# Softmax maxima turned for two chunks at once, and a second pass two rounds later

## The chip, the cores and the metric

The kernel runs on one core of a Trainium2 chip, in one launch. The time is that of one execution on the device, in microseconds (us). The core's engines work side by side, each through its own queue and in order: TensorE (PE, matrix products, with the loading of weights shown apart as PEld), VectorE (DVE), ScalarE (ACT), GpSimd (POOL) and SyncE (SP, which here only issues transfers). They wait for each other through semaphores.

## The reference

The input x has 16 sequences of 512 tokens with 256 features, in float32. One transformer block is computed, in which attention and the feed-forward part both read the same normalised input:

```python
xn = _layernorm(x, axis=-1)
x = x + _L0_attn_ref(xn, Wq, Wk, Wv, Wo) + _L0_ffn_ref(xn, router_w, router_bias, gate_w, up_w, down_w, sgate_w, sup_w, sdown_w)
```

Attention has 16 heads of 16 features, rotary embedding on q and k, a causal mask and a softmax:

```python
q, k = _rope(q, k)
scores = jnp.einsum('bqhd,bkhd->bhqk', q, k) * scale
scores = jnp.where(causal, -jnp.inf, scores)
attn = jax.nn.softmax(scores, axis=-1)
out = jnp.einsum('bhqk,bkhd->bqhd', attn, v).reshape(B, S, H * Dh)
return out @ Wo.T
```

The feed-forward part routes each of the 8192 tokens to 4 of 32 experts (gate, up and down matrices of 128 hidden features, SiLU), weighs their outputs by the softmax of the router, and adds a shared expert of 512 hidden features that every token passes.

## The kernel before

**Rounds.** The whole kernel is one list of steps that the program writes out by hand, and the engines' queues follow that order. Its beat is the round: 20 rounds a sequence, 10 for each pair p (0 and 1) of head chunks. A chunk c is four heads, laid out in 128 partitions, 32 for each head: 16 features and spare rows (`HP = 32`, `DH = 16`). `qts[b]` and `kts[b]` hold the turned q and k of sequence b with the chunks side by side, so pair p has chunks 2p and 2p+1. Sequence b begins its first pass in round 20b, and there are 320 such rounds.

**Two passes of scores.** In each round `scores(r)` (line 815) gives PE two interleaved sets of small products. The first pass multiplies q by k for two heads of one block arrangement (`BLOCKS_Q`) into the PSUM tile `sq`; DVE then takes the causal maximum of each query row (line 821, output `junk`, with the maximum itself going to `top`). The second pass works `LAG` = 10 rounds behind: k by q, turned the other way, into `sk`, where a 17th row of the operands subtracts the maximum: row `DH` of k holds -1 and row `DH` of q holds the maximum. ACT then takes the exponential (line 829, `pe`) and POOL clears what lies above the diagonal (line 841). The tiles `sq` and `sk` have one buffer each, so the next round's first pass waits until DVE has read `sq`.

**Maxima.** `maxima(b, p, c)` (lines 847 to 852) turns the four tiles `top[c]` on PE (four transposes into `pm`, line 850) and adds the result to chunk 2p+c of q on DVE (line 852, `qt<-qt,pm`). It runs for c = 0 in the pair's 8th round (20b + 10p + 7) and for c = 1 in the second round after the pair's ten (20b + 10p + 11). In the second pass the pair's chunk 0 is first read in round 20b + 10p + 10 and chunk 1 in round 20b + 10p + 14.

**Events.** Everything else of attention stands in a table of events by round: `values` (line 861, `po`, the exponentials by v), `normalized` (877 to 881, `pot`), `turned` (894, `pto`), `finish` (909, `pa`, the output projection), and for the next sequence `fetch` (line 157, the transfer of `axt`), `project` (741, `pqk`, followed on DVE by four operations of the rotary embedding, lines 751 to 761), `turn_heads` (779, `pt`) and `project_v` (769, `pv`). Each event has an estimated PE cost.

**Filling.** The feed-forward part fills the rounds. Until round 130 that is the shared expert (line 227 `psgu`, gate and up; 239 `psd`, down), from round 130 to 301 the routed experts (629 `pxt`, turn the rows; 642 `pg`, gate and up; 666 `py`, down), then the last halves of the shared expert, with the sums of the output (line 720). The routing itself runs in the first 34 rounds. The main loop gives each round as much filling as levels the estimated PE cost between two boundaries, the last of which is `full`; in a round the scores come first, then filling steps and events by turns, and events that are left over last. The gated unit behind `psgu` and `pg` costs ACT a tanh (line 260) and DVE two operations (262, 263); behind `pg` DVE also prepares the weights and numbers of the rows (`four`, `wrow`, `who`, lines 652 to 660).

```python
if r >= LAG:
    bk, sk = divmod(r - LAG, 20)
...
owed = owed + level - busy[r] if r < full else 1e9
```

Of the kernel before, what the change touches and what calls it, by code (L numbers as in the profile page):

```python
# [11 lines left out]
F32 = mybir.dt.float32  # L12
# [10 lines left out]
P = 128  # L23
# [22 lines left out]

LAG = 10
ROUNDS = B * 2 * 10  # L50
BLOCKS_Q = [[(0, 2, 0), (0, 0, 384)], [(0, 1, 0), (1, 1, 256)], [(0, 3, 0)], [(1, 3, 0)], [(1, 2, 0), (1, 0, 384)]]
BLOCKS_K = [[(0, 0, 0)], [(0, 1, 0), (0, 3, 384)], [(0, 2, 0), (1, 2, 256)], [(1, 0, 0)], [(1, 1, 0), (1, 3, 384)]]
# [17 lines left out]
def block_kernel(ctx: ExitStack, tc, x, wqkv, wo, rope, rw, rb, wexp, sg, su, sd, out):  # L70
# [64 lines left out]
    def bank(shape, name):  # L135
# [11 lines left out]
    ]  # L147

    top = [
        [fixed.tile([P, P], F32, tag=f"top{c}{i}", name=f"top{c}{i}") for i in range(NT)]  # L150
        for c in range(2)
    ]
    axts = {}

# [3 lines left out]

    def constant_heads(i):
        nc.vector.memset(qk[i], 0.0)  # L160
        nc.vector.memset(qk[i][:, NH:, DH : DH + 1], -1.0)

    def constant_values(s):
        for i in range(NT):
# [1 line left out]
            nc.gpsimd.memset(va[s][i][:, :, DH : DH + 1], 1.0)  # L166

    def constant_maxima():
        for c in range(2):
            for i in range(NT):  # L170
                nc.gpsimd.memset(top[c][i], 0.0)

    work = ctx.enter_context(tc.tile_pool(name="awork", bufs=2))

# [611 lines left out]
    def scores(r):  # L786

        jobs = []
        if r < ROUNDS:
            b, s = divmod(r, 20)  # L790
            p, s = divmod(s, 10)
            g0 = 0 if s % 2 == 0 else 2
            sq = ps_q.tile([P, 2, S], F32, tag="q", name=f"sq_{r}")
            jobs.append([
                (sq[:, h, col : col + (i + 1) * P],
                 qts[b][(g0 + h) * HP : (g0 + h) * HP + DH, 2 * p + c, i * P : (i + 1) * P],
                 kts[b][(g0 + h) * HP : (g0 + h) * HP + DH, 2 * p + c, : (i + 1) * P])
                for c, i, col in BLOCKS_Q[s // 2] for h in range(2)
            ])
        if r >= LAG:  # L800
            bk, sk = divmod(r - LAG, 20)
            pk, sk = divmod(sk, 10)
            k0 = 2 if sk % 2 == 0 else 0
            st = ps_k.tile([P, 2, S], F32, tag="k", name=f"sk_{r}")
            jobs.append([
                (st[:, h, col : col + S - k * P],
                 kts[bk][(k0 + h) * HP : (k0 + h) * HP + DH + 1, 2 * pk + c, k * P : (k + 1) * P],
                 qts[bk][(k0 + h) * HP : (k0 + h) * HP + DH + 1, 2 * pk + c, k * P :])
                for c, k, col in BLOCKS_K[sk // 2] for h in range(2)
            ])  # L810
        for n in range(max(len(job) for job in jobs)):
            for job in jobs:
                if n < len(job):
                    dst, lhsT, rhs = job[n]
                    nc.tensor.matmul(dst, lhsT=lhsT, rhs=rhs, start=True, stop=True)  # L815
        if r < ROUNDS:
            for c, i, col in BLOCKS_Q[s // 2]:
                n = (i + 1) * P
                for h in range(2):
                    at = (g0 + h) * HP + DH  # L820
                    nc.vector.tensor_tensor_reduce(  # L821
                        out=junk[:, :n], in0=sq[:, h, col : col + n], in1=causal[:, S - n :],
                        scale=1.0, scalar=LOWEST, op0=ALU.add, op1=ALU.max,
                        accum_out=top[c][i][:, at : at + 1],
                    )
        if r >= LAG:
            j = sk // 2
            pe = work.tile([P, 2, S], F32, tag="pe", name=f"pe_{r}", bufs=8)
            nc.scalar.activation(pe, st, AF.Exp, scale=DH ** -0.5)  # L829
            uncut.append((pe, j))  # L830
            pes[bk, pk, j, k0 // 2] = pe
# [12 lines left out]
                )  # L844
        uncut.clear()

    def maxima(b, p, c):
        pt = bank([P, S], f"pm_{b}_{p}_{c}")
        for i in range(NT):
            nc.tensor.transpose(pt[:, i * P : (i + 1) * P], top[c][i], ident)  # L850
        dst = qts[b][:, 2 * p + c, :]
        nc.vector.tensor_tensor(dst, dst, pt, ALU.add)

    pos_o = {}

# [94 lines left out]
    for b in range(B):  # L950
        for p in range(2):
            r = 20 * b + 10 * p
            at(r + 7, 0.45, lambda b=b, p=p: maxima(b, p, 0))
            at(r + 11, 0.45, lambda b=b, p=p: maxima(b, p, 1))
            for c, rv in ((0, r + LAG + 7), (1, r + LAG + 11)):
                at(rv, 2.3, lambda b=b, p=p, c=c: values(b, p, c))
                at(rv + 1, 0.45, lambda b=b, p=p, c=c: normalized(b, p, c))
            at(r + LAG + 13, 0.45, lambda b=b, p=p: turned(b, p))
# [185 lines left out]
```

## Time and profile before

| | us |
|---|---|
| median of 3 runs | 1840.01 |
| their range | 1839.31 to 1848.48 |
| the profiled execution's own time | 1840.64 |
| its span, first to last instruction | 1838.9 |
| PE busy | 1761.6 |
| scores, `sq` and `sk`, each matmul's mean | 0.466 and 0.467 |
| 256 transposes of maxima, busy time | 42.1 |
| 64 additions to q on DVE, busy time | 43.9 |

[...] In the timeline the columns are start, duration, engine, line, operation, output<-inputs, shape and count; a bracket at the end tells how long the engine had been idle before and what ended it. In the list of groups, the busy time and the mean in ns follow the bar, then the idle time before them. The mean granted clock of PE was 0.978.

### The profile page before, as it was taken

The numbers are of one execution on the slowest core, as the hardware profiler recorded it, in microseconds if no ns is written. First come the engines' busy times: TensorE is split into PE (matmuls) and PEld (weight loads), VectorE is DVE, ScalarE is ACT, GpSimd is POOL, SyncE is SP. The second block draws the span as 40 slices with busy tenths as digits, with TensorE's granted clock in tenths as the row PEclk, the third lists the DMA queues.
The fourth block names the chain that finished last, engine by engine and source line by source line (L and its number), as shares of the span: only waits on it lengthen the run. The fifth ranks groups of instructions, "written<-read, shape, count | busy, mean of one in ns | idle before, by whom it ended". The sixth has DMA issues, their size and how long they took to land.

```text
span 1838.9 us, 38201 instructions
## 1 busy us (share of the span) xinstructions
PE 1761.6 (96%) x13489; PEld 1297.5 (71%) x13489; DVE 1227.4 (67%) x4278; ACT 847.2 (46%) x1481; POOL 1015.9 (55%) x1336
## 2 busy tenths in 40 slices
PE   7888889999999999899999999999999999999988
PEld 5655557777776777677777787777777787777654
DVE  6888676766766666465766666666665656666784
ACT  2355433333333333255555555555555555555332
POOL 3334317767767767345666565565655665656311
PEclk9988899999999999899999999999999999999999
DMA  4644335555544433478889898888988888897797
GB/s 154 209 155 160 111 121 172 187 185 174 188 162 143 154 124 121 152 187 230 212 201 229 208 234 206 224 208 209 238 200 230 208 217 223 200 247 159 204 305 235
DMA packets 230832, 353.24 MB, mean 192 GB/s; under 512 B 23408, under 2 KB 166512, under 8 KB 230640
## 3 DMA queue, kind: packets, MB, share of 16 engines
q1 hardware_dynamic: 168176, 262.83, 45.2%
q0 software_dynamic: 55296, 76.86, 21.4%
q10 hardware_dynamic: 7168, 11.09, 1.7%
q8 instruction: 107, 1.75, 0.4%
q14 instruction: 85, 0.70, 0.1%
HBM read 220.74 MB, written 131.01 MB: 191 GB/s over the span
## 4 chain that ended last, share of the span: by engine, by line
PE 85%; DVE 9%; DMA 2%; ACT 2%; issue 1%; SPq 1%; ACTq 0%; POOL 0%; DVEq 0%
PE pg L642 15%; PE sq L815 13%; PE psgu L227 11%; PE po L861 7%; PE py L666 7%; PE pqk L741 5%; PE psd L239 5%; PE sk L815 4%; PE pxt L629 4%; PE pt L779 3%; PE pa L909 3%; PE pv L769 3%; DVE junk L821 2%; PE pm L850 2%; PE pot L877 1%
## 5 line engine op out<-in xcount | busy, mean ns | idle before, releaser
L680 POOL DMA_INDIRECT moe<-yb,who x288 | 449.9, 1562 | 301.5 <-DMA moe<-yb,who 120.1
L821 DVE CUSTOM_DVE_ANT_0 junk<-sq,causal 128x384 bf16<-128x384 f32 (+3 forms) x1024 | 502.8, 491 | 153.3 <-PE sk L815 117.7
L829 ACT ACTIVATE pe<-sk 128x1024 f32<-128x1024 f32 x320 | 327.8, 1024 | 332.0 <-PE sk L815 264.8
L841 POOL TENSOR_SCALAR_AFFINE_SELECT pe<-pe 128x256 f32<-128x256 f32 x512 | 262.5, 641 | 271.1 <-ACT pe L829 268.3
L815 PE MATMUL sq<-kt,qt 16*128 16x384 f32 (+3 forms) x2048 | 369.8, 466 | 18.6 <-DVE top L821 18.5
L815 PE MATMUL sk<-qt,kt 17*128 17x512 f32 (+3 forms) x2048 | 369.9, 467 | 1.8 <-ACT pe L829 1.8
L535 POOL DMA_INDIRECT xs<-rows,pos x256 | 250.6, 979 | 82.6 <-issue 66.9
L642 PEld LDWEIGHTS pg<-xbt,w 128*128 128x128 f32 x2304 | 275.4, 193 | 26.8 <-ACT yb L674 9.4
L642 PE MATMUL pg<-xbt,w 128*128 128x128 f32 x2304 | 289.8, 279 | 2.5 <-DMA w<-in_wexp 2.5
L815 PEld LDWEIGHTS sq<-kt,qt 16*128 16x128 f32 x2048 | 175.9, 186 | 147.8 <-issue 41.6
L815 PEld LDWEIGHTS sk<-qt,kt 17*128 17x128 f32 x2048 | 176.3, 186 | 10.2 <-ACT pe L829 2.8
L262 DVE SCALAR_TENSOR_TENSOR gs_e<-th_e,pg 128x256 f32<-128x256 f32 x144 | 60.7, 421 | 169.8 <-ACT th_e L260 160.0
L861 PE MATMUL po<-pe,va 128*32 128x512 f32 (+3 forms) x2048 | 157.3, 449 | 0.0
L666 PE MATMUL py<-w,ht 128*128 128x256 f32 x576 | 152.3, 387 | 0.0
L227 PE MATMUL psgu<-sxt,sg_sb 128*128 128x256 f32 x496 | 140.9, 408 | 4.9 <-DMA sxt<-xt_d 3.3
L674 ACT ACTIVATE yb<-py,wrow 128x256 f32<-128x256 f32 x288 | 121.3, 474 | 31.9 <-PE py L666 31.4
L227 PE MATMUL psgu<-sxt,su_sb 128*128 128x256 f32 x496 | 131.5, 389 | 0.0
L861 PEld LDWEIGHTS po<-pe,va 128*32 128x32 f32 x2048 | 61.2, 112 | 99.6 <-issue 78.3
L260 ACT ACTIVATE th_e<-pg 128x256 f32<-128x256 f32 x144 | 55.3, 384 | 160.6 <-PE pg L642 160.6
L239 PE MATMUL psd<-sd_sb,hs 128*128 128x256 f32 x512 | 127.2, 392 | 0.4 <-DVE hs L263 0.4
L260 ACT ACTIVATE th_s<-psgu 128x256 f32<-128x256 f32 x128 | 49.1, 384 | 159.3 <-PE psgu L227 154.6
L227 PEld LDWEIGHTS psgu<-sxt,sg_sb 128*128 128x128 f32 x496 | 89.3, 196 | 38.5 <-issue 15.7
(148 smaller groups left out, 2491.1 us busy)
## 6 DMA issues: line engine op xcount, KB each, us to landing
w<-in_wexp SPq DMA_DIRECT2D x288, 384.5 KB
xb<-xs SPq DMA_DIRECT2D x144, 265.0 KB
sum<-moe SPq DMA_DIRECT2D x48, 256.0 KB
xn_d<-xn SPq DMA_DIRECT2D x16, 530.0 KB
rows<-xn_d SPq DMA_DIRECT2D x16, 530.0 KB
xt_d<-xt ACTq DMA_DIRECT2D x32, 256.0 KB
moe<-none SPq DMA_DIRECT2D x16, 512.0 KB
sxt<-xt_d SPq DMA_DIRECT2D x31, 256.0 KB
```

The costliest lines, as they stand in the source:

```text
L227: nc.tensor.matmul(ps[:, u, :], lhsT=w[:, c, m * P : (m + 1) * P], rhs=hold["xt"][:, c, :], start=(c == 0), stop=(c == 1),)
L239: nc.tensor.matmul(hold["py"][:, il, :], lhsT=hold["h"][:, m, il * P : (il + 1) * P], rhs=sd_sb[:, m, :], start=(m == 0), stop=(m == HS // ...
L535: nc.gpsimd.indirect_dma_start(out=views[n % NVIEWS], out_offset=bass.IndirectOffsetOnAxis(ap=index, axis=0), in_=row, in_offset=None,)
L642: nc.tensor.matmul(pg[:, u, c * HB : (c + 1) * HB], lhsT=w[n][:, c, at : at + H], rhs=rows[:, dc, c * HB : (c + 1) * HB], start=(dc == 0), ...
L666: nc.tensor.matmul(py[:, c, :], lhsT=h[:, c * P : (c + 1) * P], rhs=w[n][:, c, 2 * D : 3 * D], start=True, stop=True,)
L674: nc.scalar.mul(yb[:, c, :], py[:, c, :], weight[:, c : c + 1])
L680: nc.gpsimd.indirect_dma_start(out=moe[c], out_offset=bass.IndirectOffsetOnAxis(ap=at[:, c : c + 1], axis=0), in_=yb[:, c, :], in_offset=N ...
L815: nc.tensor.matmul(dst, lhsT=lhsT, rhs=rhs, start=True, stop=True)
L821: nc.vector.tensor_tensor_reduce(out=junk[:, :n], in0=sq[:, h, col : col + n], in1=causal[:, S - n :], scale=1.0, scalar=LOWEST, op0=ALU.a ...
L829: nc.scalar.activation(pe, st, AF.Exp, scale=DH ** -0.5)
L841: nc.gpsimd.affine_select(out=diag, in_=diag, compare_op=ALU.is_ge, fill=0.0, base=0, pattern=[[0, 2], [1, P]], channel_multiplier=-1,)
L861: nc.tensor.matmul(po[g * HP : (g + 1) * HP, k * P :], lhsT=va[b % 2][k][:, 8 * p + 4 * c + g, :], rhs=pes[b, p, j, g // 2][:, g % 2, col ...
```

## The change

Both chunks of a pair now share one set of tiles. The maxima of chunk c go to column `DH + c` of a head's 32, so four transposes turn both chunks, and one addition adds both rows to both chunks of q. Chunk c of k has its -1 in row `DH + c` and zero in the other, so that each chunk subtracts its own maximum; the second pass reads 18 rows. `top` is now kept by pair instead of by chunk. The single call per pair is in round 20b + 10p + 11, after all ten rounds of its first pass. The second pass runs 12 rounds behind, and `values`, `normalized`, `turned` and `finish`, which are placed by `LAG`, move by two rounds with it. The next sequence's `fetch`, `project`, `turn_heads` and `project_v` get other rounds, and the boundary `full` is written by `LAG` (328; it was 326).

```diff
-LAG = 10
+LAG = 12
...
-        nc.vector.memset(qk[i][:, NH:, DH : DH + 1], -1.0)
+        chunks = qk[i][:, NH:, :].rearrange("p (k h) e -> p k h e", h=4)
+        for c in range(2):
+            nc.vector.memset(chunks[:, c::2, :, DH + c : DH + c + 1], -1.0)
...
-                 kts[bk][(k0 + h) * HP : (k0 + h) * HP + DH + 1, 2 * pk + c, k * P : (k + 1) * P],
-                 qts[bk][(k0 + h) * HP : (k0 + h) * HP + DH + 1, 2 * pk + c, k * P :])
+                 kts[bk][(k0 + h) * HP : (k0 + h) * HP + DH + 2, 2 * pk + c, k * P : (k + 1) * P],
+                 qts[bk][(k0 + h) * HP : (k0 + h) * HP + DH + 2, 2 * pk + c, k * P :])
...
-                    at = (g0 + h) * HP + DH
+                    at = (g0 + h) * HP + DH + c
...
-                        accum_out=top[c][i][:, at : at + 1],
+                        accum_out=top[p][i][:, at : at + 1],
...
-    def maxima(b, p, c):
-        pt = bank([P, S], f"pm_{b}_{p}_{c}")
+    def maxima(b, p):
+        pt = bank([P, S], f"pm_{b}_{p}")
         for i in range(NT):
-            nc.tensor.transpose(pt[:, i * P : (i + 1) * P], top[c][i], ident)
-        dst = qts[b][:, 2 * p + c, :]
-        nc.vector.tensor_tensor(dst, dst, pt, ALU.add)
+            nc.tensor.transpose(pt[:, i * P : (i + 1) * P], top[p][i], ident)
+        dst = qts[b][:, 2 * p : 2 * p + 2, :]
+        nc.vector.tensor_tensor(dst, dst, pt.unsqueeze(1).to_broadcast([P, 2, S]), ALU.add)
...
-            at(r + 7, 0.45, lambda b=b, p=p: maxima(b, p, 0))
-            at(r + 11, 0.45, lambda b=b, p=p: maxima(b, p, 1))
+            at(r + 11, 0.45, lambda b=b, p=p: maxima(b, p))
...
-            at(20 * b + 6, 0.0, lambda b=b: fetch(b + 1))
-            for i, r in enumerate((9, 12, 15, 19)):
+            at(20 * b + 7, 0.0, lambda b=b: fetch(b + 1))
+            for i, (r, rv) in enumerate(((10, 22), (12, 24), (16, 25), (18, 26))):
...
-                at(20 * b + 22 + i, 0.9, lambda b=b, i=i: project_v(b + 1, i))
+                at(20 * b + rv, 0.9, lambda b=b, i=i: project_v(b + 1, i))
...
-    last, full = ROUNDS + LAG + 16, ROUNDS + 6
+    last, full = ROUNDS + LAG + 16, ROUNDS + LAG - 4
```

More of the change, by code (lines that the diff above doesn't have):

```diff
@@ L149, in block_kernel @@
     top = [
-        [fixed.tile([P, P], F32, tag=f"top{c}{i}", name=f"top{c}{i}") for i in range(NT)]
-        for c in range(2)
+        [fixed.tile([P, P], F32, tag=f"top{p}{i}", name=f"top{p}{i}") for i in range(NT)]
+        for p in range(2)
     ]
@@ L168, in constant_maxima @@
     def constant_maxima():
-        for c in range(2):
+        for p in range(2):
             for i in range(NT):
-                nc.gpsimd.memset(top[c][i], 0.0)
+                nc.gpsimd.memset(top[p][i], 0.0)
     work = ctx.enter_context(tc.tile_pool(name="awork", bufs=2))
```

## The prediction

> **What bounds the kernel now.** I read the page's busy times first, then the same by stage, then single rounds in the timeline.
>
> ```profile
> span 1838.9 us, 38201 instructions
> PE 1761.6 (96%) x13489; PEld 1297.5 (71%) x13489; DVE 1227.4 (67%) x4278; ACT 847.2 (46%) x1481; POOL 1015.9 (55%) x1336
> ```
>
> TensorE (PE) works 96% of the span, VectorE (DVE) 67%. The next view splits the span at the stages: before the 34th round, with the shared expert as filling, with the routed experts, rounds 302 to 319. Columns: window, time, then busy us of PE, PEld, DVE, ACT, POOL, granted clock, DMA share, GB/s.
>
> ```profile
> 37.30:261.00 223.70, 189.18 (x1345) 127.80 (x1344) 172.65 (x736) 100.47 (x207) 77.83 (x231) 0.90 0.43 143
> 261.00:770.00 509.00, 498.48 (x3436) 356.05 (x3432) 345.15 (x1046) 180.86 (x277) 343.21 (x441) 0.99 0.48 159
> 770.00:1704.00 934.00, 931.21 (x7776) 718.90 (x7780) 593.46 (x2202) 512.98 (x918) 551.92 (x557) 0.99 0.85 214
> 1704.00:1787.00 83.00, 73.81 (x555) 51.02 (x548) 64.82 (x177) 28.54 (x41) 18.97 (x34) 0.96 0.83 259
> ```
>
> In the two long stages (1443 us) PE is all but never idle (498.48 of 509, 931.21 of 934): a microsecond of PE work removed there is a microsecond won, a microsecond of PE waiting added is one lost. At the two ends DVE is the busier of the two for its stage (77% and 78%) and PE has gaps. The third view is one round of the expert stage, round 167.
>
> ```profile
> 974.20 0.69 PE L815 MATMUL sq<-kt,qt 16*128 16x512 f32 x1
> ...
> 975.27 2.05 PE L642 MATMUL pg<-xbt,w 128*128 128x128 f32 x16
> 975.40 0.69 DVE L821 CUSTOM_DVE_ANT_0 junk<-sq,causal 128x512 bf16<-128x512 f32 x1 [0.49 <-PE sk L815]
> ...
> 976.75 0.08 DVE L821 DVE_READ_ACCUMULATOR2_ANT top<- 128x1 f32 x1
> ...
> 977.26 2.36 PE L861 MATMUL po<-pe,va 128*32 128x512 f32 x32
> ...
> 977.84 0.42 DVE L262 SCALAR_TENSOR_TENSOR gs_e<-th_e,pg 128x256 f32<-128x256 f32 x1 [1.01 <-ACT th_e L260]
> ...
> 979.10 0.17 DVE L660 COPY who<-xb 128x2 int32<-128x2 int32 x1
> ...
> 979.55 0.66 PE L629 MATMUL pxt<-ident,xb 128*128 128x128 f32 x4
> ...
> 980.04 0.60 PE L850 MATMUL pm<-ident,top 128*128 128x128 f32 x4
> ...
> 980.57 0.18 PEld L815 LDWEIGHTS sq<-kt,qt 16*128 16x128 f32 x1 [0.17 <-issue]
> ...
> 980.68 0.69 DVE L852 TENSOR_TENSOR qt<-qt,pm 128x512 f32<-128x512 f32 x1 [1.41 <-PE pm L850]
> ```
>
> It holds PE's prices, from start to next start: the round's scores 1.07 us (974.20 to 975.27), values 2.29, the transposes of maxima 0.53 here (0.44 to 0.45 where a like set of four follows another). Likewise in other rounds: pg 1.78, py 0.87, four pxt 0.44, one psgu 1.73, half a psd 0.91, pqk 1.72; joins between blocks add about 0.2 us a round (166: scores, pg, pxt, py sum to 4.16, the round took 4.35). It also shows DVE's clockwork when pg comes right after the scores: maxima done 2.6 us after the round's start (3.0 with four pieces), then gate work until 979.27, which is 5.07 us after it. And it shows L852, the addition to q, ending at 981.37, 0.8 us after the next round's scores have begun. Today nobody misses it: those rows are read three rounds later.
>
> **The change part by part.** *Maxima once per pair.* 32 of the 64 sets of four transposes go: 32 x 0.45 = 14.4 us of PE (by 0.44 and 0.53: 14.1 to 17.0). One wide addition of 128x1024 stands for two of 128x512. No row has that shape; these bound it:
>
> ```profile
> L850 PE MATMUL pm<-ident,top 128*128 128x128 f32 x256 | 42.1, 287 | 0.0
> L852 DVE TENSOR_TENSOR qt<-qt,pm 128x512 f32<-128x512 f32 x64 | 43.9, 687 | 60.0 <-PE pm L850 59.9
> L881 DVE TENSOR_TENSOR ot<-pot,rs 128x256 f32<-128x256 f32 x64 | 27.2, 424 | 2.2
> ```
>
> Doubling 256 to 512 adds 263 ns, so 1024 takes 687 + 2 x 263 = 1213 ns; below lies 687 (nothing for the second half), above 2 x 687 = 1374. I take 1.21. The 18th row of the second pass is free: 16 and 17 rows cost the same 1.07 us.
>
> *Lag twelve.* Two more rounds hold the first pass alone and two more the second alone. A round with one pass still took 1.06 us in the trace, so 332 instead of 330 blocks cost 2 x 1.06 = 2.1 us. Together PE's work falls by 12.3 us.
>
> *The new wait.* This is the heart. The addition is issued in round 20b+11 (first pair) or 20b+21 (second), and the second pass of that pair begins in the very next round; before there were three rounds between. The second matmul in PE's queue for that round needs the whole addition, PE works in order, and behind it stand the rest of the scores and all that follows. On DVE the addition is queued behind the round's maxima and behind the gate work of any block that PE was given before the transposes. In the first pair's case a projection was also issued one round earlier (pqk is last in round 20b+10). What this costs DVE is seen in round 170, whose scores began at 991.45:
>
> ```profile
> 991.21 0.69 DVE L751 TENSOR_TENSOR tcos<-pqk,rope_sb 128x512 f32<-128x512 f32 x1
> ...
> 992.89 0.62 DVE L761 TENSOR_TENSOR qk<-tcos,tsin 128x256 f32<-128x256 f32 x1
> 993.44 0.55 DVE L821 CUSTOM_DVE_ANT_0 junk<-sq,causal 128x384 bf16<-128x384 f32 x1
> ...
> 995.18 0.08 DVE L821 DVE_READ_ACCUMULATOR2_ANT top<- 128x1 f32 x1
> ```
>
> The maxima end 3.8 us into that round instead of 3.0; with pqk last they end at about 3.95. So I go through the 32 places with the order in which the changed program issues its instructions, compare when DVE ends (plus 0.1 for the signal) with when PE comes to the next scores, and call the difference the stall.
>
> Expert stage, 18 places. Second pair, pg ahead of the transposes: gate work to 5.07, addition to 6.3, scores possible at 6.4; PE (scores, pg, pxt, pm, py, joins) is there at 4.8: 1.6 us each in rounds 141, 261, 281; in 301 py comes twice, 1.2; in 241 another pg covers it. First pair, pg ahead: 3.95 + 1.45 gate work + 1.21 + 0.1 = 6.7 against 4.8: 1.9 each in 211 and 231, 0.1 in 191 under another pg. First pair, no pg ahead: 5.25, and up to 0.75 more where gate work of the round before is queued ahead of the projection, against 4.4 to 5.67: 0.7 (131), 0.75 (151, 291), 1.05 (171), 0.8 (271), none in 251. Second pair, no pg ahead (161, 181, 201, 221): 4.3 against 4.8 or more, none. Sum 14.0 us. If the addition took 0.69 it would be about 8, with 1.37 and the slower rows of the gate work (0.75 for 0.35) about 20.
>
> Shared stage, 9 places, psgu in pg's stead (gate work ends at 4.4): 1.35 (61), 0.55 (81, 121), 0.65 (41), none (101), 0.9 (51, 91), 0.95 (71, 111): 6.8 us, 3 to 10 by the same bounds.
>
> Start, 3 places (11, 21, 31). There the routing's DVE work (some 3 us) stands ahead of the addition too; gross 2.5 to 5 us each, but PE already loses about 45 us in these rounds to such chains, and one delay hides another. I take 4, bounds -4 and 12.
>
> End. In rounds 305 to 319 DVE, with the sums of the output, is the slower engine, so that the same work of PE spread over two more rounds leaves more for after round 320: 6 us more PE work there by the order, 2.5 less before; I take 2 (0 to 6). Rounds 311 and 321 have only psgu and psd around the transposes: 2 us of waiting each, 4 (0 to 7).
>
> *Moved steps.* The load of axt is issued a round later, and so is its first reader, three rounds on as before; it waits for the last project_v, one round earlier in both. On SP it passes a round's stores and loads, none of which waits for it. turn_heads writes the other kt one round after its last reader instead of two, in PE's own order. I cost these at nothing: three rounds are over 14 us; if the load were late, up to 5 us a sequence.
>
> Sum: -14.4 + 2.1 + 14.0 + 6.8 + 4 + 2 + 4 = +18.5 us on the profiled execution's 1840.64 us (span 1838.9 and 1.7 around it), 0.63 above the median shown: 1858.5 for the median; I say 1858.
>
> [...]
>
> **The rivals.** *The saving shows, the wait does not* (20%): the addition runs earlier than I queue it, or PE's joins swallow the lateness. For it: PE has 0.8 us pauses that nobody explains, and DVE is 36% idle there. Against: DVE works in order and the rows above leave it 1 to 2 us late. Price: 1840.0 - 14.4 + 2.1 = 1828. The point that decides is the sum of stalls: under 3.1 us the change is faster by over 0.5%.
> *It cancels* (18%): stalls between 3.1 and 21.5 us, because the start and the end give nothing and the expert stage is at its lower bound, 8 + 3: 1839; with the evener spread of values, projections and finishes some of PE's present gaps before the scores go as well.
> *The ends get worse* (12%, slower too): DVE-bound rounds at both ends pay in full, 12 + 13 us for my 10: 1873.
> *Forecast* (50%): 1846 to 1870.
>
> **The numbers.** 0.5% (9.2 us) is about what a measurement of this kernel can tell from no change. Faster 0.20, within 0.18, slower 0.62. The range goes from the saving's case, 1829, to 1871; the likeliest case has 1846 to 1870.
>
> **What would show it.** In the changed profile: pm x128 and about 14 us less; the addition near 1.21 us; the waits of second-pass scores (sk) on DVE's qt, near nothing now, at some 20 us or more in about 20 places, the rounds after 20b+11 and 20b+21 lengthened where pg stands before pm; PE no longer 100% busy in the expert stage. Were sk to wait for qt under 5 us in all, my prediction is wrong and the time falls to 1828.

## The result and the profile after

The changed kernel took 1897.97 us in the median of four runs (1892.49 to 1902.74) against 1839.66 of the kernel before beside it (1837.45 to 1848.48): 1.0296 times as long, 95% interval 1.0268 to 1.0323. It is slower, as forecast, but by 58 us where 18.5 had been worked out, and lies above the stated range, which ended at 1871 us.

First the busy times of the changed kernel's page, then busy times by stage: before round 34, the shared expert as filling (to round 130), the routed experts (to round 302), rounds 302 to 319, the rest. Columns: window, time, busy us of PE, PEld, DVE, ACT, POOL, granted clock, DMA share, GB/s.

```profile
span 1896.2 us, 37958 instructions
PE 1788.5 (94%) x13361; PEld 1311.4 (69%) x13361; DVE 1220.2 (64%) x4248; ACT 844.0 (45%) x1481; POOL 1013.9 (53%) x1336
```

```profile
37.00:276.00 239.00, 193.77 (x1266) 126.57 (x1268) 169.48 (x722) 94.41 (x199) 74.59 (x225) 0.84 0.39 132
276.00:795.00 519.00, 502.80 (x3428) 361.08 (x3430) 342.08 (x1032) 182.35 (x282) 342.93 (x442) 0.99 0.47 156
795.00:1745.00 950.00, 939.55 (x7737) 723.64 (x7733) 593.30 (x2200) 512.54 (x920) 550.05 (x557) 0.99 0.85 211
1745.00:1834.00 89.00, 76.10 (x524) 50.95 (x526) 64.35 (x175) 28.09 (x41) 21.70 (x35) 0.90 0.79 245
1834.00:1896.20 62.20, 51.46 (x304) 31.54 (x296) 27.94 (x55) 17.32 (x22) 9.98 (x20) 0.88 0.61 200
```

The same cut through the kernel before, first, fourth and fifth stage:

```profile
37.30:249.50 212.20, 180.95 (x1297) 121.43 (x1296) 168.81 (x725) 97.51 (x202) 77.06 (x229) 0.90 0.44 148
...
1706.30:1789.20 82.90, 73.71 (x533) 51.03 (x532) 66.22 (x182) 28.02 (x41) 18.32 (x34) 0.96 0.85 267
1789.20:1838.90 49.70, 41.52 (x257) 24.32 (x256) 26.06 (x49) 14.71 (x19) 8.10 (x16) 0.92 0.75 238
```

PE has 128 matmuls fewer and is busy 27 us longer. In the first stage it ran 31 matmuls fewer and was still busy for 12.8 us more, at a granted clock of 0.84 instead of 0.90; it was idle 45 us and not 31. In the trace the granted clock of PE stands at half in blocks of 3.4 us. Such blocks make up 41 us of the first stage before and 75 after, and 15 and 32 us from round 302 on; in the two long stages they are the same, 24 us together.

Against the prediction by stage, with round starts from both traces and the prediction's PE work split by the order in which the programs issue it:

| stage | before | after | change | predicted |
|---|---|---|---|---|
| to round 34 | 249.5 | 275.8 | +26.3 | +1.8 (work -2.2, waits 4) |
| to round 130 | 515.2 | 518.9 | +3.7 | +1.1 (work -5.7, waits 6.8) |
| to round 302 | 941.5 | 950.2 | +8.7 | +6.4 (work -7.6, waits 14.0) |
| to the end | 132.6 | 151.2 | +18.6 | +9.2 (work 3.2, 2 + 4 for the end) |

The two long stages, where nearly all of the working went, came out 5 us above the forecast. The two short ends hold 45 of the 57 us.

The wait itself is there. This is the group of the new addition in the changed kernel (duration in ns as min/median/max), with what waited for it:

```profile
L855 DVE TENSOR_TENSOR qt<-qt,pm x32: 1208/1216/1222, 116.4 to 1842.0; 128x1024 f32<-128x1024 f32 x32
its engine sat idle before it (us, times) until:
  PE pm L853: 1.0, 2
who waited for it (us, times):
  PE sk L818: 17.4, 11
  PEld sk L818: 9.5, 3
```

The addition took 1.216 us for 1.21 predicted, and second-pass scores on PE waited for it 17.4 us at 11 places (PEld's 9.5 us are mostly two of the same waits, in rounds 12 and 22, seen at the loading of weights). One such place, round 232, in the timeline:

```profile
1353.29 0.49 PE L853 MATMUL pm<-ident,top 128*128 128x128 f32 x3
...
1355.01 0.69 PE L818 MATMUL sq<-kt,qt 16*128 16x256 f32 x2
1355.05 0.42 DVE L266 SCALAR_TENSOR_TENSOR ht<-gs_e,pg 128x256 f32<-128x256 f32 x1
...
1355.39 0.35 DVE L655 SCALAR_TENSOR_TENSOR four<-xb,w 128x4 f32<-128x4 f32 x2
...
1355.92 1.21 DVE L855 TENSOR_TENSOR qt<-qt,pm 128x1024 f32<-128x1024 f32 x1
...
1357.28 0.66 PE L818 MATMUL sk<-qt,kt 18*128 18x512 f32 x1 [1.58 <-DVE qt L855]
```

The transposes ended at 1353.8, but DVE came to the addition only at 1355.92, after the maxima and the gate work of a block (gs_e, ht, four). PE started the round at 1355.01, issued one pair of first-pass matmuls and stood until 1357.28, 0.15 us after the addition's end: scores longer by 2.27 us. That is the mechanism as predicted.

### The profile page after: what moved, and what is told of

The parts are those of the page before. It is cut to its first block, busy times and chain, and to the rows that moved or that the text cites. A ratio compares the mean times of both kernels' runs of the same rounds, so it can differ in the third digit from the quotient of the medians.

```text
span 1896.2 us, 37958 instructions
## 1 busy us (share of the span) xinstructions
PE 1788.5 (94%) x13361; PEld 1311.4 (69%) x13361; DVE 1220.2 (64%) x4248; ACT 844.0 (45%) x1481; POOL 1013.9 (53%) x1336
## 4 chain that ended last, share of the span: by engine, by line
PE 80%; DVE 11%; DMA 3%; ACT 2%; issue 2%; SPq 1%; POOL 0%; ACTq 0%; DVEq 0%; POOLq 0%
PE pg L645 14%; PE sq L818 11%; PE psgu L230 10%; PE py L669 7%; PE po L864 7%; PE pqk L744 6%; PE sk L818 5%; PE psd L242 5%; PE pxt L632 3%; PE pt L782 3%; PE pv L772 3%; PE pa L912 3%; DVE junk L824 2%; DMA sum<-moe 1%; PE pot L880 1%
## 5 line engine op out<-in xcount | busy, mean ns | idle before, releaser
L844 POOL TENSOR_SCALAR_AFFINE_SELECT pe<-pe 128x256 f32<-128x256 f32 x512 | 267.1, 657 | 289.4 <-ACT pe L832 288.6
L818 PE MATMUL sq<-kt,qt 16*128 16x384 f32 (+3 forms) x2048 | 385.2, 470 | 20.5 <-DVE top L824 19.7
L818 PE MATMUL sk<-qt,kt 18*128 18x512 f32 (+3 forms) x2048 | 371.9, 468 | 19.6 <-DVE qt L855 17.4
L818 PEld LDWEIGHTS sq<-kt,qt 16*128 16x128 f32 x2048 | 182.8, 187 | 162.1 <-issue 58.4
L818 PEld LDWEIGHTS sk<-qt,kt 18*128 18x128 f32 x2048 | 177.8, 187 | 50.3 <-issue 11.9
L669 PE MATMUL py<-w,ht 128*128 128x256 f32 x576 | 153.8, 390 | 0.7 <-DVE four L655 0.5
L242 PE MATMUL psd<-sd_sb,hs 128*128 128x256 f32 x512 | 132.2, 403 | 0.6 <-DVE hs L266 0.5
L744 PE MATMUL pqk<-wqkv_sb,axt 128*128 128x512 f32 x240 | 119.8, 624 | 0.2 <-ACT qt L787 0.2
```

What stands on the lines that cost most here:

```text
L242: nc.tensor.matmul(hold["py"][:, il, :], lhsT=hold["h"][:, m, il * P : (il + 1) * P], rhs=sd_sb[:, m, :], start=(m == 0), stop=(m == HS // ...
L669: nc.tensor.matmul(py[:, c, :], lhsT=h[:, c * P : (c + 1) * P], rhs=w[n][:, c, 2 * D : 3 * D], start=True, stop=True,)
L744: nc.tensor.matmul(pqk, lhsT=axts[b][:, c, tok], rhs=wqkv_sb[:, c, : 2 * D], start=(c == 0), stop=(c == 1),)
L844: nc.gpsimd.affine_select(out=diag, in_=diag, compare_op=ALU.is_ge, fill=0.0, base=0, pattern=[[0, 2], [1, P]], channel_multiplier=-1,)
```

## The experiments

Each number after a label is the ratio to the kernel before, run in the same set, with its interval. The sets ran on different chips. The kernel before took 1840 to 1844 us in the sets of the result and of the fourth below, and 1877 to 1887 us in the others; there its shared stage above all was longer (547.8 for 515.2 us in one profile) and its expert stage by 4.6 us, so stages are compared mainly by the start and the end, where it repeated within 2.3 us. "Lengthening" is the time from the first score of a round to the first matmul that is not a score, over the 1.07 us it takes undisturbed, summed over the rounds that end in 2: in the changed kernel 11.9, 3.3, 12.4 and 2.8 us by stage, before 2.0 and then next to nothing.

**Set 1: one part at a time.**

```diff
e1_max10: the changed kernel, transposes and addition a round earlier
-            at(r + 11, 0.45, lambda b=b, p=p: maxima(b, p))
+            at(r + 10, 0.45, lambda b=b, p=p: maxima(b, p))
e2_oldproj: the changed kernel with the old rounds of the next sequence's steps
-            at(20 * b + 7, 0.0, lambda b=b: fetch(b + 1))
-            for i, (r, rv) in enumerate(((10, 22), (12, 24), (16, 25), (18, 26))):
+            at(20 * b + 6, 0.0, lambda b=b: fetch(b + 1))
+            for i, (r, rv) in enumerate(((9, 22), (12, 23), (15, 24), (19, 25))):
e3_lag12: the kernel before with the lag alone
-LAG = 10
+LAG = 12
-    last, full = ROUNDS + LAG + 16, ROUNDS + 6
+    last, full = ROUNDS + LAG + 16, ROUNDS + LAG - 4
e4_newproj: the kernel before with the new rounds of fetch, project, project_v alone
```

> The changed kernel with the one call of maxima a round earlier (20b+10p+10 instead of +11), so that a whole round lies between the addition to q and the first second-pass scores that read it. If the new wait explains the loss, nearly all of the lengthening of the scores in rounds 20b+12 and 20b+22 goes (it adds up to about 30 us over all stages in the changed kernel, 12 of them in the expert stage), and the time falls from 1898 by 20 to 30 us, to 1868 to 1878. If the new rounds of the projections and the values are the larger cause, the scores' lengthening goes too, but the start keeps its 26 us and the time stays at 1885 or more.

> The changed kernel with the fetches, projections, turns of heads and value projections in their rounds from before (6; 9, 12, 15, 19; two later; 22 to 25). If the start lost its 26 us because all projections now stand in even rounds, behind the routing's products, while the odd rounds are left short, most of it comes back: the 34th round begins by 260 us instead of 276, and the time is 1870 to 1880. If it was the wait for the addition alone, the start stays at 270 or more and the time at 1890 or more (the first pair's addition has no projection just ahead any more, which is worth some 5 us by itself).

> The kernel before with the second pass twelve rounds behind and the boundary of the filling moved with it, two calls of maxima as before. By work on TensorE alone this costs 2 us (two more rounds of scores), and by the prediction's reckoning of the end 2 to 6 more: 1842 to 1848. If the values that the lag moves into round 303 wait there for GpSimd, and idle stretches at the end run at half clock, the end alone costs 10 to 18 us and the time is 1850 to 1858.

> The kernel before with only the new rounds of fetch, projections, turns and value projections (7; 10, 12, 16, 18; two later; 22, 24, 25, 26). If their place behind the routing's products is what slows the start, the 34th round begins 10 to 20 us later than 249.5 and the time is 1850 to 1860. If the wait for the addition is the whole matter, nothing changes beyond 3 us: 1837 to 1843.

| run | ratio | to 34 | to 130 | to 302 | to the end | half clock to 34 |
|---|---|---|---|---|---|---|
| e1_max10 | 1.0130 (1.0059 to 1.0201) | 273.7 | 545.1 | 939.7 | 150.1 | 71.7 |
| e2_oldproj | 1.0063 (1.0025 to 1.0101) | 260.2 | 547.8 | 942.6 | 153.2 | 58.0 |
| e3_lag12 | 1.0038 (1.0005 to 1.0072) | 254.9 | 542.4 | 946.0 | 146.1 | 54.6 |
| e4_newproj | 1.0181 (1.0097 to 1.0265) | 264.0 | 561.7 | 953.9 | 133.4 | 61.4 |

With a whole round between addition and reader, all lengthening is gone, and the expert stage falls by 10.5 us against the changed kernel's 950.2; the start gains only 2 us. The old rounds of the projections bring the start from 275.8 to 260.2. The lag alone lengthens the end by 13.5 us and saves nothing. The new rounds alone, put into the kernel before, cost 1.8%: some 13 us at the start, 7.8 in the expert stage and more in the shared one, against the kernel before as it ran in set 2; they leave the end as it was. The step that the prediction cost at nothing is the dearest of all.

Why, the waits between 90 and 250 us show (columns: engine, line, releaser, us in total, times, longest). Before, then changed:

```profile
ACT wt L421 <- DVE wt L418: 21.9, 11, 4.5
PEld pl L390 <- ACT xt L382: 21.5, 20, 3.4
...
PE pl L390 <- ACT xt L382: 16.0, 19, 3.2
```

```profile
PEld pl L393 <- ACT xt L385: 32.5, 20, 3.9
ACT wt L424 <- DVE wt L421: 26.2, 10, 3.3
PE pl L393 <- ACT xt L385: 25.9, 18, 3.7
```

In the even rounds of the first 34, PE's queue holds the router's transposes (ptx), the router's product (pl), which waits for ACT's copies xt, and only behind it the projections. The copies come late because ACT, in order, first waits for the end of the routing chain on DVE (wt) to take its exponential. The changed kernel puts all four projections and all four of the turns that follow them into even rounds, behind that wait. Round 16 of the changed kernel:

```profile
152.55 0.66 PE L393 MATMUL pl<-xt,rw_sb 128*32 128x128 f32 x8 [2.81 <-ACT xt L385]
153.53 0.66 PE L393 MATMUL pl<-xt,rw_sb 128*32 128x128 f32 x8 [0.33 <-ACT xt L385]
154.12 3.71 PE L744 MATMUL pqk<-wqkv_sb,axt 128*128 128x512 f32 x4
```

PE waits 2.81 us for xt, and the projection behind it takes 3.71 us (3.64 from start to next start) while the granted clock stands at half, for 1.72 from start to next start at the full one: beside the wait, 1.92 us more for the same work. The round took 11.2 us; the same round before, with no projection in it, 5.5. Summed over rounds 10 to 32, the even rounds took 83.3 us before, 111.1 in the changed kernel and 105.4 in e4_newproj; the odd rounds 9 to 33 took 79.1, 77.0 and 71.6. What is lost is in the even rounds, 27.8 and 22.1 us, and the odd ones give only 2.1 and 7.5 us back.

**Set 2: other rounds for the projections, and both kernels as they are.**

```diff
e5_odd: the changed kernel with
+            for i, (r, rv) in enumerate(((11, 22), (13, 24), (17, 25), (19, 26))):
e6_mix: the changed kernel with
+            for i, (r, rv) in enumerate(((11, 22), (15, 24), (17, 25), (21, 26))):
+            at(r + 10, 0.45, lambda b=b, p=p: maxima(b, p))
+R_LAST = 304
```

> The changed kernel with the four projections (and the turns of heads, two rounds behind them) a round later: 11, 13, 17, 19 in place of 10, 12, 16, 18, so that they stand in odd rounds, behind the router's logits and not behind the routing's products of the even ones. If even against odd is what costs the start, the start comes down by 10 to 15 us against the changed kernel, and the other stages change by under 5: 10 to 18 us faster than it. If the distance to the addition and its wait matter more, the start stays within 4 us.

> The changed kernel with three places mended: maxima a round earlier (20b+10p+10), projections in odd rounds away from the values (11, 15, 17, 21), and the end of the expert stage two rounds later (304), so that the values of round 303 stand in it. If the wait, the parity of the projections and the two rounds at the end are the three causes, it loses about 30 (wait), 15 (start) and 8 (round 303) of the 57 us and lands within 0.5% of before, on either side; if the two more rounds themselves cost the end, 10 us of it stay. If the three causes aren't the whole, it stays 25 us or more above before.

> The kernel before once more, to have its trace from the same chip as the next three. Every theory expects its stages as at first (about 250, 515, 942 and 133 us to the boundaries at rounds 34, 130, 302 and the end), longer in the shared stage by some 27 us if this chip is the one on which the four kernels of the first set ran.

> The changed kernel once more on this chip: slower than before by 40 to 60 us, with the start some 26 us and the end some 18 us longer than before's and the scores of rounds 20b+12 and 20b+22 lengthened by about 30 us in all. If the 26 us of the start were a matter of the chip, they shrink to under 10.

| run | ratio | to 34 | to 130 | to 302 | to the end |
|---|---|---|---|---|---|
| b_again (before) | profile only | 251.8 | 547.8 | 946.1 | 132.6 |
| a_again (changed) | 1.0190 (1.0127 to 1.0252) | 276.9 | 539.0 | 949.5 | 151.7 |
| e5_odd | 1.0217 (1.0167 to 1.0267) | 263.4 | 549.0 | 961.0 | 150.8 |
| e6_mix | 1.0205 (1.0148 to 1.0261) | 258.4 | 566.8 | 949.3 | 147.2 |

Both e5_odd and e6_mix miss in time and hit by half: in odd rounds the projections do give the start 13.5 and, with the wait taken out too, 18.5 us back. The rest goes out again later. With lag twelve the values stand in rounds that end in 3 and 9, and both edits put a turn of q and k there that the very next round reads (in rounds 19 of 20, and in e6_mix 3 of 20 too). In e6_mix the next scores then wait on PE for ACT's copies of k, 33 us in all between rounds 40 and 299, for ACT copies the values first; in e5_odd the trace shows little of this wait, and its round 19 also holds a projection more. Averaged over rounds 40 to 299, round 3 of each 20 took 7.3 us in e6_mix and 5.4 in a_again, round 19 took 6.9 and 6.4 in e6_mix and e5_odd for 5.3. In e5_odd round 13 took 8.1 for 5.7, with values that wait for POOL (10.8 us on PE). The kernel before leaves two full rounds between such a turn and its reader. The parity of the round was one cause; what else stands in the round, and the distance to the reader, are others.

**Set 3: two undone at once, the addition in halves, an odd lag, the end.**

```diff
f1_split: the changed kernel
-        dst = qts[b][:, 2 * p : 2 * p + 2, :]
-        nc.vector.tensor_tensor(dst, dst, pt.unsqueeze(1).to_broadcast([P, 2, S]), ALU.add)
+        for c in range(2):
+            dst = qts[b][:, 2 * p + c, :]
+            nc.vector.tensor_tensor(dst, dst, pt, ALU.add)
f2_undo2: the edits of e1_max10 and e2_oldproj together
f3_lag11: f2_undo2 and f1_split, with LAG = 11, R_LAST = 303, full = ROUNDS + 6
f4_end: the changed kernel with R_LAST = 304, full = ROUNDS + 6
```

> The changed kernel with its one addition of 128x1024 made in two of 128x512, the first chunk's half first; the first two rounds of a second pass read that half alone. Theory (PE's second-pass scores wait for the end of the addition they read): every lengthening of scores in rounds 2 mod 10 is 0.5 us shorter, which takes the expert stage's 12.4 us to about 7, the shared stage's 3.2 to about 1 and the start's 11.9 to about 10; the kernel 7 to 10 us faster than the changed kernel, about 1.4% slower than the kernel before if the changed one is 1.9% slower there. Rival (the scores wait for all of q's tile, whichever half they read): two additions end 0.17 us later than one, expert stage at 13 to 15 us, the kernel equal to the changed one or up to 4 us slower.

> The changed kernel with the transposes and addition one round earlier (r+10, so that a whole round lies before the first reader) and with the rounds of load, projections and values' projections of the kernel before. Left of the change: maxima of both chunks at once, and the lag of twelve. Theory (wait, moved projections and lag are three costs that add up): no lengthening of scores in rounds 2 mod 10; 14.4 us of PE saved, 2.1 of scores added, some 4 us more at the start and 13 to 18 more from round 302 on, so +3 to +8 us against the kernel before (ratio 1.002 to 1.005), start stage 250 to 256 us, end 146 to 150. Rival (each delay taken away is replaced by the next, as at the start where the scores' wait gave way to waits for ACT): 1.006 or more, start stage 260 or more.

> Maxima of both chunks at once with a lag of eleven instead of twelve: transposes in r+10, first reader in r+11, the addition in two halves, the rounds of load and projections of the kernel before, the shared expert's last work spread to round 326 as in the kernel before, the sums' stage begun at round 303 so that the values of round 302 stand ahead of the block additions that GpSimd has left. Theory: -14.4 + 1 of PE, waits of the scores for the addition some 7 us in the expert stage, 1 to 2 in the shared one and 3 at the start, 3 to 5 us more at the end: -2 to +4 us against the kernel before (ratio 0.999 to 1.002); end stage (from round 302) 134 to 142 us. Rival (a lag other than ten costs what twelve costs, whatever is around it): 1.006 or more, end stage 146 or more.

> The changed kernel with two edits at its end only: the sums' stage begun at round 304 instead of 302, which puts the values of round 303 ahead of the block additions still in GpSimd's queue, and the shared expert's last work spread to round 326 instead of 328. Theory (the end lost 5 us of waiting in round 303 with half a clock behind it, and 8 us of PE work that was moved behind round 326): wait of po for GpSimd in 303 gone, time from round 302 to the end 151 -> 138 to 144 us, the kernel 7 to 13 us faster than the changed kernel; start and expert stage as in the changed kernel. Rival (DVE, with the sums, sets the end whatever PE's order): end stays at 147 to 152 us, the kernel within 4 us of the changed one.

| run | ratio | to 34 | to 130 | to 302 | to the end |
|---|---|---|---|---|---|
| f1_split | 1.0166 (1.0116 to 1.0217) | 280.4 | 539.1 | 941.9 | 145.8 |
| f2_undo2 | 0.9943 (0.9914 to 0.9972) | 251.2 | 533.3 | 933.9 | 149.3 |
| f3_lag11 | 1.1311 (1.1257 to 1.1365) | 293.8 | 591.3 | 1088.9 | 147.2 |
| f4_end | 1.0211 (1.0163 to 1.0259) | 275.3 | 540.6 | 942.8 | 153.8 |

f1_split: the lengthening in the expert stage fell from 12.4 to 5.8 us (7 expected) and the stage by 8 us; smaller pieces helped there. In the whole, where 7 to 10 us had been expected, the gain is within the intervals.

f2_undo2: no lengthening, the start back at 251.2 and only the end still long. The ratio, 0.9943, is below the 1.002 to 1.005 of the theory, and the rival's 1.006 is further off. At the start the two costs had hidden each other: undone one at a time they give 2.1 and 15.6 us back, together 24.6.

f3_lag11 lies far beyond both theories. First and second pass use alternate pairs of heads, and by an even lag the two passes of a round are on different pairs; an odd lag puts both on the same pair. PE's scores of one round in f3_lag11, then the first of a round in f2_again (the text of f2_undo2):

```profile
955.10 0.92 PE L818 MATMUL sq<-kt,qt 16*128 16x384 f32 x4
955.85 0.82 PE L818 MATMUL sk<-qt,kt 18*128 18x384 f32 x4
956.50 0.49 PE L818 MATMUL sq<-kt,qt 16*128 16x128 f32 x4
956.72 0.49 PE L818 MATMUL sk<-qt,kt 18*128 18x128 f32 x4
```

```profile
828.89 0.58 PE L818 MATMUL sq<-kt,qt 16*128 16x384 f32 x1
828.90 0.58 PE L818 MATMUL sk<-qt,kt 18*128 18x384 f32 x1
828.91 0.58 PE L818 MATMUL sq<-kt,qt 16*128 16x384 f32 x1
828.91 0.58 PE L818 MATMUL sk<-qt,kt 18*128 18x384 f32 x1
```

In the second, four matmuls of four heads start within 0.02 us of each other; in the first the sk of a shape begin 0.75 and 0.22 us after the sq of the same shape, and a round's scores took 2.0 us instead of 1.07. Over f2_undo2 its first three stages were 43, 58 and 155 us longer, the scores alone 25, 79 and 157: in the expert stage they are the whole of it. With heads assigned to rounds as here the lag has to be even, which left open what a lag of eleven would do for the end.

f4_end: the wait in round 303, shown below in the changed kernel, was gone, and the end was no shorter. Its rounds 307, 308 and 312 took 8.1, 7.6 and 9.5 us for 5.0, 5.5 and 5.2 in the changed kernel. PE waited 5.0 us for DVE's maxima at the end of round 307, with half clock in 308, and in 312 for maxima and the addition, 1.0 and 1.1 us. The rival, an end set by DVE, held for the whole kernel (within 4 us of the changed one) and nearly for the end (153.8 us for 147 to 152). But before the 5.0 us DVE itself had stood 3.9 us for the load of rows to be summed (`sum<-moe`): it was late by standing in its order for that load, and not only by the amount of its work.

```profile
1749.99 1.56 POOL L683 DMA_INDIRECT moe<-yb,who  x1 [0.85 <-ACT va L776]
...
1754.49 1.56 POOL L683 DMA_INDIRECT moe<-yb,who  x1 [0.94 <-DMA moe<-yb,who]
1755.49 2.05 POOL L844 TENSOR_SCALAR_AFFINE_SELECT pe<-pe 128x256 f32<-128x256 f32 x4
1756.53 0.20 PEld L864 LDWEIGHTS po<-pe,va 128*32 128x32 f32 x8 [5.84 <-POOL pe L844]
1756.53 2.79 PE L864 MATMUL po<-pe,va 128*32 128x384 f32 x24 [4.93 <-POOL pe L844]
```

The values of round 303, two rounds later than before through the lag, need a masked block that POOL comes to only after the block additions queued when round 302 closed the expert stage. PE stood 4.9 us; rounds 303 and 304 took 9.8 and 7.2 us, before 3.1 and 3.9.

**Set 4: the end, and the best so far once more.**

```diff
f2_again: f2_undo2 once more, nothing changed
g1_last300: f2_undo2, g2_after300: the changed kernel, g3_before300: the kernel before, these three with
-R_LAST = 302
+R_LAST = 300
```

> The text of f2_undo2 once more, as the base of the next run on the same chip: 0.991 to 0.998 of the kernel before.

> f2_undo2 with the sums' stage begun at round 300 instead of 302, so that GpSimd's left-over block additions are behind it before the values of round 303 and the sums keep their distance to the second pass. Theory (the end lost its time to that meeting and to sums two rounds late): the wait of po for GpSimd in round 303 gone, 7 to 14 us faster than f2_again, ratio to the kernel before 0.986 to 0.991. Rival (VectorE's sums set the end whatever is moved): within 3 us of f2_again, new waits for DVE after round 306.

> The changed kernel with the sums' stage begun at round 300 instead of 302 and nothing else. Theory: wait in round 303 gone, 7 to 14 us faster than the changed kernel (ratio to the kernel before 1.012 to 1.016 where the changed kernel has 1.019). Rival: within 3 us of it.

> The kernel before with the sums' stage begun at round 300 instead of 302 and nothing else. Theory (the meeting of values and left-over block additions is what costs): its values of round 301 now stand right behind those additions, po waits some 5 us for GpSimd there and the time from round 300 to the end grows by 5 to 10 us, ratio 1.002 to 1.006. Rival (beginning the sums earlier is a gain by itself, whatever the lag): 0.994 to 0.998.

| run | ratio | to 34 | to 130 | to 302 | to the end |
|---|---|---|---|---|---|
| f2_again | 1.0048 (1.0024 to 1.0071) | 251.1 | 513.2 | 934.4 | 149.7 |
| g1_last300 | 1.0065 (1.0035 to 1.0096) | 251.4 | 511.9 | 952.9 | 141.5 |
| g2_after300 | 1.0356 (1.0306 to 1.0406) | 277.6 | 517.6 | 956.8 | 147.8 |
| g3_before300 | 1.0051 (1.0028 to 1.0074) | 255.3 | 515.1 | 953.6 | 137.2 |

The stage's start moved, and a wait moved along: round 301 took 8.3 us in g3_before300 and 9.5 in g1_last300. In the first PE stood 1.65 us for a masked block behind POOL's additions, as the theory said, though not for the 5 us that it named; in the second the wait on POOL was gone and PE stood 2.92 us for the load of the shared expert's input (`sxt`), with the clock at half behind it. What the end won, the rounds before it lost, and the changed kernel got no faster. g3_before300 came out at the ratio that its theory gave, g1_last300 and g2_after300 did not, and f2_again missed its forecast of 0.991 to 0.998. So the end's loss through the lag is shown (e3_lag12, f2_again), and the wait in 303 is one part of it; that moving this wait away does not win it back is shown three times (f4_end, g1_last300, g2_after300).

How the 17.1 us of f2_again's end divide, its trace shows. PE was idle for 10.0 us more than in the kernel before (27.4 for 17.4): 6.3 us for POOL in round 303, and 3.6 in round 326 for DVE's gate work, for which DVE had come late after standing 4.9 us for a load of rows to be summed; the waits for DVE's maxima stayed at 8.6 us for 8.0. PE was busy for 7.1 us more: the order puts 3.5 us of work there (a set of values and two rounds of scores more, two sets of transposes fewer), and 6.4 us more of its work ran at half clock, by an estimate of half of that 3.2 us (a projection took 3.64 us from start to next start at half clock for 1.72, in round 16 above).

f2_again is the cleanest account of the change, since the kernel before ran here as it did in the result:

```profile
37.00:251.00 214.00, 181.69 (x1263) 118.23 (x1260) 168.50 (x721) 93.39 (x198) 75.41 (x225) 0.89 0.43 147
251.00:764.00 513.00, 502.91 (x3433) 362.47 (x3429) 339.43 (x1032) 183.54 (x282) 341.89 (x442) 0.98 0.48 158
764.00:1699.00 935.00, 927.55 (x7738) 717.49 (x7740) 590.74 (x2200) 510.25 (x920) 550.08 (x558) 1.00 0.86 214
1699.00:1787.00 88.00, 72.30 (x520) 48.40 (x521) 63.91 (x174) 28.18 (x41) 22.18 (x35) 0.92 0.82 248
1787.00:1848.50 61.50, 49.77 (x304) 30.68 (x296) 28.43 (x55) 17.32 (x22) 8.78 (x20) 0.91 0.62 202
```

Against the kernel before: start +1.6, shared -2.0, experts -7.1, end +17.1. The transposes saved do show in the expert stage once wait and projections are out of the way. By the matmuls in the two traces it holds 17 sets of transposes of maxima fewer (7.7 us), one set of values fewer, which now stands behind round 302 (2.3 us), and 0.45 us more for outputs: 9.5 us less work, of which 7.1 show. The end then takes more than all stages gave.

**Set 5: the pairing without the lag.**

```diff
h1_lag10: f2_undo2 and f1_split with LAG = 10, full = ROUNDS + 6, and
+            at(r + 9, 0.45, lambda b=b, p=p: maxima(b, p))
```

> Maxima of both chunks at once with the lag of ten and the rounds of load and projections of the kernel before: transposes in r+9, the last round of the pair's first pass, the addition in two halves, the first reader in r+10. Theory (the lag costs the end, the pairing itself costs only the wait of the first reader): end stage 131 to 136 us as in the kernel before, 14.4 us of PE saved, waits for the maxima of the same round and for the addition of some 0.5 us at 32 places, 10 to 18 us in all: -4 to +4 us against the kernel before, ratio 0.997 to 1.003. Rival (the wait at the end of the first pass is much longer, since the transposes now stand behind the maxima of their own round on VectorE): 1 us or more at each place, ratio 1.008 or more.

It gave 1.0105 (1.0065 to 1.0146), with stages of 254.9, 561.6, 959.7 and 135.7 us. The end is back within 3.1 us of the kernel before; with e3_lag12 that shows that the lag is what the end pays for. The ratio is the rival's; the group of the transposes shows its wait:

```profile
its engine sat idle before it (us, times) until:
  DVE top L824: 35.4, 24
```

The transposes stand in the round whose maxima they need, and PE, in order, waits for them. The 35.4 us count the matmuls and the loading of their weights, which stand for the same maxima; the matmuls alone waited 21.9 us at 13 of the 32 places, 1.7 us each, where the rival had 1 us or more at every place. Rounds that end in 9 took 6.69 us on average in the expert stage, before 5.60. Only f2_undo2 came out faster than the kernel before at all, by 0.6% where that took 1880 us; where it took 1844 us the same text was 0.5% slower.

## Why the prediction was wrong, by its own steps

*PE's saving, -14.4 + 2.1:* right in kind, hidden in the changed kernel. f2_again shows 7.1 of the 9.5 us that its order takes out of the expert stage, and only 2.0 of the 4.1 in the shared one.

*The new wait, 14.0 and 6.8:* the mechanism, the duration of the addition and, in the expert stage, most of the places were right: 1.5 us measured for 1.6 in rounds 142, 262 and 282, 1.8 and 2.3 for 1.9 in 212 and 232, nothing where none was expected. Measured lengthening was 12.4 us in the expert stage, but 3.3 in the shared one, half of what was expected there; taking the wait out (e1_max10) was worth 10.5 us of the expert stage. Over all stages the rounds that end in 2 lengthened by 30.3 us (2.3 before), where 14.0 + 6.8 + 4 + 4 = 28.8 had been expected. That these sums agree is partly luck, since the start's share was 11.9 us for 4 and made up for the others. The mechanism of this term was not what failed.

*Moved steps, "I cost these at nothing":* this is the step that failed. It asked whether the load would be late and whether a buffer would be free, and not what stands ahead of the moved matmuls in PE's queue. Of the start's 26.3 us, 15.6 went when only these rounds were undone (e2_oldproj), another 9.0 when the wait was undone with them (f2_undo2), while the wait alone gave 2.1 (e1_max10); 1.7 are left. It was not the start alone: the expert stage fell from 950.2 to 942.6 us with these rounds undone, and grew by 7.8 us with the new rounds alone (e4_newproj). The prediction took 4, with bounds of -4 and 12, for the start's wait and nothing for the moves. "One delay hides another" was right: behind the projections' delay the wait cost little of its own. The 45 us that PE was said to lose in the start already is too much: the prediction's own row leaves it 34.5 us idle there.

*The clock:* no term had it. The prediction read 0.90 in the start's window and 0.99 in the long stages, and took every lost microsecond at one. Half-clock time in the trace grew by 34 us at the start and 17 at the end, and in it PE was busy for 25.7 and 15.4 us more; by an estimate of half of each, from the projection's 3.64 us for 1.72, 12.9 and 7.7 us of that is work that only took longer. It is a share of the same 26.3 and 18.6 us, not a further term: with wait and moves undone, half-clock time at the start was back at 41.0 us in f2_undo2 and 47.8 in f2_again. The trace of the changed kernel has 25 slow stretches, of 3.4, 6.8 or 10.2 us, which all begin on one grid of 3.41 us; in the 3.4 us ahead of each, PE and its loads had stood for 1.95 us in the median, for 0.6 at least, and for over 3 us in only three cases. Under which condition the clock falls, these figures do not show.

*The end, 2 + 4:* mis-sized. Beside 3.2 us of work by the order it allowed 6 us, where 15.4 of the 18.6 were left to explain. It named PE work shifted past round 320 and two waits. The lag alone made 13.5 us (e3_lag12), 5.6 of them a wait on POOL in round 303, which the prediction did not have: it went through DVE's queue for the addition, but not through POOL's for the values that the lag moved. It also called DVE the busier of the two at both ends; its own rows have PE at 85% and 89% there and DVE at 77% and 78%.

*The rivals:* the sum of stalls was far above the 3.1 us under which the saving would have shown, and the case that it cancels fell with it. "The ends get worse" had the right place, with 25 us where 45 were lost, and another cause for the larger part: 15.6 us of the start came back when nothing but the moved rounds was undone (e2_oldproj).

*One addition or two:* the prediction worked with one addition of 1.21 us. Two halves (f1_split) shortened the waits by 6.6 us in the expert stage, and the kernel's median by less than its interval.

## What to carry to other kernels

Price a moved step by the queue that it lands in: list what stands ahead of it on its engine in the new round and what that waits for, on every engine whose result it or its readers need, above all in the short stages at the ends where engines wait for each other. Count beside PE's pauses what the granted clock adds: here the start was 14 us more idle and, at a granted clock of 0.84 for 0.90, 12.8 us longer busy with no more matmuls. And a saving of work spread evenly over a kernel is easily outweighed by what its schedule must do to get it: here 14 us of transposes less were bought with two rounds of lag that cost 17.

## What the runs showed of the hardware

A round's scores took 1.07 us with first and second pass on different heads, where the matmuls of four heads start within 0.02 us of each other (f2_again), and 2.0 us with both on the same pair of heads, where those of sk begin 0.75 us after those of sq (f3_lag11). That kernel took 13% longer than the one before, 157 us of it in the scores of the expert stage alone.

The same program, with nothing changed, took 1839 us in one profile and 1878 in another. 32.6 of the 39.4 us were in the shared stage, 515.2 and 547.8 us, in fourteen of its 96 rounds. In some of them several engines stood for something outside what the profile shows:

```profile
ACT oc L868 <- remote: 6.3, 1, 6.3
...
DVE qt L852 <- remote: 3.4, 1, 3.4
...
DVE junk L821 <- remote: 2.3, 1, 2.3
```

In such a set the changed kernel's loss was 1.9% instead of 3.0%, mostly since its own shared stage lengthened less (518.9 to 539.0 us). What the engines stood for is open.
